# Where one transfer stands in a convolution kernel: the kept rows of VectorE's layout, written behind the next shifts of the 3x3 part

## The chip, the cores and the metric

The kernel runs on one core of a Trainium2 chip. The time is device microseconds of one execution of the whole program; the time of a kernel is the median of its runs. The core has TensorE (PE, matrix products), VectorE (DVE), ScalarE (ACT), GpSimd (POOL) and SyncE (SP). They run at the same time, each through its own list of instructions in order, and wait for each other by semaphores. SP and POOL issue the transfers (DMAs); SP does nothing else here.

## What is computed

`x` holds 8 images of 32 channels and 128 x 128 pixels, in float32. Layer 0 normalises them by groups, finds for every pixel the 8 most similar of 25 shifted copies, gathers those into 256 channels, and runs them through three pairs of a 1x1 and a 3x3 depthwise convolution. Layer 1 is a 5x5 convolution.

```
xb = _patch_match_stack(x)                      # [8, 256, 128, 128]
dct = _conv(xb, dct_w, groups=C)
h = relu(_conv(_conv(xb, w1), w2, groups=CK, pad=1))
h = relu(_conv(_conv(h, w3), w4, groups=CK, pad=1))
wiener = sigmoid(_conv(_conv(h, w5), w6, groups=CK, pad=1))
filt = _conv(wiener * dct, inv_dct_w, groups=C)
...
x = x + _L0_conv_ref(_gn(x), ...)
x = x + _L1_conv_ref(_gn(x), L1_conv_kernel, 1, 2)
```

The change concerns the 3x3 depthwise convolutions (`w2`, `w4`, `w6`).

## The kernel before

**Steps and phases.** An image is cut into strips of 8 rows; a step handles one strip, and each image has 16 strips and a last short one (`n == NS`), so 17 steps, 136 in all. In every step the main loop passes through four phases, `i` = 3, 2, 1, 0. Phases 3, 2 and 1 run a stage, that is one pair of 1x1 and 3x3 convolutions, each on a strip that entered a step later than the one before; phase 0 multiplies by the `dct` part and closes a strip. The gathering of pixels, the block matching for the next image (task queues drained by `run` and `tick`) and layer 1 are spread between.

**Two layouts for a 3x3 part.** A stage has 256 channels. The first 128 go through PE: `pointwise_t` makes the 1x1 part into the tile `t` (one for each stage), ACT copies it from PSUM (L668), and two transfers on SP's queue, L671 and L673, shift rows between partitions so that PE finds the three neighbouring rows side by side. `depthwise_t` then does the nine taps as 48 small matmuls (L709). The second 128 go through DVE: `pointwise_v` makes the 1x1 part, ACT copies it into `tv` (L646), `depthwise_v` does the centre tap on ACT (L686) and the eight others on DVE (L689), then the activation function on ACT (L693).

**Rows kept from strip to strip.** A 3x3 part needs two rows of the strip above. `rows_before_t` (L617) and `rows_before_v` (L624) transfer them inside `t` and `tv`: for `tv`, rows 8 and 9 go to rows 0 and 1. Both are on SP's queue. At the end of an image they write zeros on POOL instead (L619, L626). The taps of a strip must have read rows 0 and 1 before they are overwritten, and L646 of the next strip must not write rows 2 to 9 before rows 8 and 9 are read.

**How the pieces of a phase are written.** `depthwise_v` and `depthwise_t` are generators; the main loop takes a piece of each at a time. In phase `i`, in this order: `pointwise_v` of the stage and the centre tap; the eight taps on DVE (`next(new_v, None)`); `pointwise_t` with its shifts; the matmuls L709 of the stage of the phase before (`next(dt, None)`), after the gathering matmuls or, in phase 0, ahead of them; then the end of the stage of the phase before: `next(dv, None)` gives L693 and the kept rows of `tv`, `next(dt, None)` gives ACT's L721 and the kept rows of `t`.

**What sets the order.** The loop stands under a manual schedule for PE, DVE and ACT: these three run in the written order. SP and POOL are not in that set:

```
ORDERED = {mybir.EngineType.PE, mybir.EngineType.DVE, mybir.EngineType.Activation}
...
    with tc.manual_schedule(engines=ORDERED):
```

Their order is made by the framework's planner, which knows what each instruction reads and writes and in which order all were written, and which also sets the semaphores.

Of the kernel before, what the change touches and what calls it, by code (L numbers as in the profile page):

```python
# [43 lines left out]
def bm3d_conv_preact(  # L44
# [171 lines left out]
    def push(task):  # L216
        want = next(task, None)
        if want:
            which, cost, *wait = want
            queues[which].append((cost, task, now[0] + (wait[0] if wait else 0)))  # L220
# [400 lines left out]
    def rows_before_v(i, b, n):  # L621
        v = tv[i - 1]
        if n < NS:
            nc.sync.dma_start(v[:, 0:2], v[:, R : R + 2])  # L624
        else:
            nc.gpsimd.memset(v[:, 0 : i + 1], 0.0)  # L626
# [21 lines left out]
    def pointwise_t(i, b, n, lhsT, src):  # L648
        t = tb[i - 1]
        nb = 2 if n < NS else 1  # L650
        if n == NS and i == 1:
            nc.gpsimd.memset(t[:, :, 2], 0.0)
        else:
            for q in range(2):
                ps = ps_x.tile([P, 2, 2, W], F32, name=f"p{i}_{b}_{n}_{q}", tag="x")
                for e in range(2):
                    s = slice(C * (2 * q + e), C * (2 * q + e + 1))
                    for g in range(2):
                        rows = src(g)
                        for r in range(4):  # L660
                            nc.tensor.matmul(  # L661
                                ps[C * r : C * (r + 1), e, :nb],
                                lhsT[:, g, s],
                                rows[:, r : r + 4 * nb - 3 : 4],
                                start=g == 0,
                                stop=g == 1,
                            )
                nc.scalar.copy(t[:, 2 * q : 2 * q + 2, 2 : 2 + nb], ps[:, :, :nb])  # L668
            for r in range(i - 1) if n == 0 else range(i - 1, 4) if n == NS else ():
                nc.gpsimd.memset(t[C * r : C * (r + 1), :, 2], 0.0)  # L670
        nc.sync.dma_start(t[64:P, :, 0:nb], t[0:64, :, 2 : 2 + nb])  # L671
        if nb == 2:
            nc.sync.dma_start(t[0:64, :, 1], t[64:P, :, 2])  # L673

    def depthwise_v(i, b, n):
        v = tv[i - 1]
        nr = R if n < NS else 4
        out_ = accp.tile([P, R, W], F32, name=f"acc{i}_{b}_{n}_1", tag=f"acc{i}1")
        acc = out_[:, :nr]
        for k, (dy, dx) in enumerate(  # L680
            ((1, 1), (0, 0), (0, 1), (0, 2), (1, 0), (1, 2), (2, 0), (2, 1), (2, 2))
        ):
            tap = dwv[:, i - 1, 3 * dy + dx : 3 * dy + dx + 1]
            rows = v[:, dy : dy + nr, dx : dx + W]
            if k == 0:
                nc.scalar.activation(acc, rows, AF.Copy, scale=tap)  # L686
                yield out_
            else:
                nc.vector.scalar_tensor_tensor(  # L689
                    acc, rows, tap, acc, op0=ALU.mult, op1=ALU.add  # L690
                )
        yield
        nc.scalar.activation(acc, acc, funcs[i - 1])  # L693
        rows_before_v(i, b, n)

    def depthwise_t(i, b, n):
# [28 lines left out]
    def final_load(b, n):  # L725
        j0, j1 = (3, R) if n == 0 else (0, R if n < NS else 3)
        ya, yz = R * n - 3 + j0, R * n - 3 + j1

        whole = j1 - j0 == R
        nr, nw = (2, W) if whole else (j1 - j0, C)  # L730
        xr = work.tile([P, 2 * W], F32, name=f"xr_{b}_{n}", tag="xr")
        xr = xr[:, : nr * nw].rearrange("p (r w) -> p r w", w=nw)
        for j in range(4):
            ra = ya + 2 * j if whole else ya
            xa = 0 if whole else C * j
            nc.gpsimd.dma_start(
                xr[C * j : C * (j + 1)], x[b, :, ra : ra + nr, xa : xa + nw]
            )

        xf = xbp.tile([P, 2, R, W], F32, name=f"xf_{b}_{n}", tag="xf", bufs=1)  # L740
        src = xbd[b].rearrange("(j m c) g y x -> g m j c y x", j=4, m=2)
        for g in range(2):
            for m in range(2):
                nc.gpsimd.dma_start(
                    xf[64 * g : 64 * (g + 1), m, j0:j1], src[g, m, :, :, ya:yz]
                )
        return xr, xf, j0, j1
# [119 lines left out]
    def unit(stage, u):  # L867
        if 0 <= u < len(units) and units[u]:
            stage(*units[u])

    def source(i, b, n):
        src = xbs.pop((b, n), None) if i == 1 else accs.pop((i - 1, b, n))
        return (lambda g: src[:, g]) if i == 1 else (lambda g: src[g])
# [9 lines left out]
    def tick(i):  # L883

        now[0] += 1
        owed[0] += total / (NS - 2) * (0.4 if i == 0 else 0.2)
        owed[0] -= run("D", owed[0]) if owed[0] > 0 else 0
        owed[0] = min(owed[0], 6.0)

    def until(cond, credit):  # L890
        while not cond():
            now[0] += 1
            run("D", credit)
            run("A")
            run("P")
            run("Q")

    with tc.manual_schedule(engines=ORDERED):
        push(prep(0))
        push(mixes())  # L900
        until(lambda: 0 in ready, 4.0)
        xbd[0] = dram.tile([P, 2, H, W], F32, name="xbd_0", tag="xbd")
        for i in range(3):
            nc.gpsimd.memset(tb[i][0:64, :, 0], 0.0)
        for u in range(7):
            unit(gather_load, u)
            unit(gather_select, u - 2)
            unit(gather_pixels, u - 3)
        u = 4

        dt = dv = iter(())

        later = lambda: None

        for s in range(len(steps) + 2):
            if s < len(steps):
                b, n = steps[s]
                if s == 2:
                    push(bands())
                if n == 0 and b + 1 < NB:  # L920
                    push(prep(b + 1))
                if n == NS - 1 and b + 1 < NB:
                    until(lambda: b + 1 in ready, 4.0)
                    xbd[b + 1] = dram.tile([P, 2, H, W], F32, name=f"xbd_{b+1}", tag="xbd")
            for i in (3, 2, 1, 0):
                si = s - (i - 1 if i else 2)
                live = 0 <= si < len(steps)
                new_v = new_t = iter(())
                if live:
                    bi, ni = steps[si]  # L930

                if live and i:
                    src = source(i, bi, ni)
                    pointwise_v(i, bi, ni, lws[i - 1], src)
                    new_v, new_t = depthwise_v(i, bi, ni), depthwise_t(i, bi, ni)
                    accs[i, bi, ni] = [None, next(new_v)]
                later()
                later = lambda: None
                if live and not i:
                    if ni == 0:  # L940
                        x1d[bi] = dram.tile([C, H, W], F32, name=f"x1d_{bi}", tag="x1d")
                        stats[bi] = work.tile([P, NS + 1, 6], F32, name=f"stat_{bi}", tag="stat")
                    xr, xf, j0, j1 = fins.pop(si)
                run("P")
                if live and not i:
                    final_dct(bi, ni, accs[3, bi, ni], xf, j0, j1)

                run("Q")
                if s < len(steps):
                    unit(gather_select, u + 1)  # L950
                    unit(gather_load, u + 3)
                    tick(i)
                next(new_v, None)
                if live and i:
                    pointwise_t(i, bi, ni, lws[i - 1], src)
                if not i:
                    next(dt, None)
                if s < len(steps):
                    unit(gather_pixels, u)
                    u += 1  # L960
                if i:
                    next(dt, None)
                run("A")
                next(dv, None)
                next(dt, None)
                dv, dt = new_v, new_t
                if live and not i:
                    later = partial(end, bi, ni, xr, j0, j1)
                if not i and 0 <= s - 1 < len(steps):
                    fins[s - 1] = final_load(*steps[s - 1])  # L970
        later()
        until(lambda: NB - 1 in done, 4.0)

# [61 lines left out]
```

## Time and profile before

| | us |
|---|---|
| median of 3 runs | 7167.68 (7158.68 to 7188.37) |
| profiled execution | 7169.27 |
| its span, first to last instruction | 7167.5 |
| DVE taps, L689, 3264 of them | 4083.7 busy, 1.252 each |
| PE 3x3 matmuls, L709, 19584 of them | 2174.5 busy |
| shifts L671 and L673 with kept rows L617, issue to landing | 4.9 median |
| kept rows L624, issue to landing | 4.0 median, 2.0 to 12.4 |

A line of the waits view tells who waited and in which line, after the arrow what ended the wait, then microseconds in total, how many times, and the longest. "SPq" is the queue of SP: its instructions wait in order, so one that waits holds all that stand behind it. A line of the timeline gives start, duration, engine, line, operation and tiles; "x8" means eight instructions merged. The groups' busiest lines read thus:

```profile
L689 DVE SCALAR_TENSOR_TENSOR acc<-tv,dwv,acc 128x1024 f32<-128x1024 f32 (+1 forms) x3264 | 4083.7, 1252 | 214.6 <-ACT acc L686 103.2
L709 PE MATMUL pw<-t,dwd 128*32 128x508 f32 (+6 forms) x19584 | 2174.5, 591 | 151.3 <-DMA t<-t 116.0
```

That is busy time and mean duration in ns, then the idle time ahead of the group and what ended most of it.

### The profile page before, as it was taken

How to read it: one execution, taken by the hardware profiler on the slowest of the kernel's cores; microseconds unless marked ns; L12 is line 12 of the kernel's file. 1: busy time of each engine (PE TensorE's matmuls, PEld its weight loads, DVE VectorE, ACT ScalarE, POOL GpSimd, SP SyncE). 2: the span in 40 equal slices, each digit the busy share in tenths (PEclk: the TensorE clock that was granted, in tenths of full speed). 3: DMA queues.
4: the chain of work that ended last, by engine and by line, in shares of the span. 5: the costliest groups of instructions: out<-in, count | busy, mean ns of one | idle time of the engine just before them, and what ended most of it. 6: DMA issues, size and time to landing. Idle time of an engine off the chain costs nothing. (4 is left out here: it accounts for less than half of the span.)

```text
span 7167.5 us, 229467 instructions
## 1 busy us (share of the span) xinstructions
PE 6709.5 (94%) x100226; PEld 3178.5 (44%) x100226; DVE 5835.6 (81%) x8606; ACT 5061.9 (71%) x6704; POOL 2716.4 (38%) x4599
## 2 busy tenths in 40 slices
PE   4699999999999999999999999999999999999997
PEld 1344444444444444444444444444444444444443
DVE  7689878788788888888888888888888889767675
ACT  4777668677686777767677776877668677676662
POOL 6343335333353333533344333543335333232222
PEclk7799999999999999999999999999999999999999
DMA  3476656667566665756656565666656655556652
GB/s 82 120 163 146 149 136 152 139 148 152 131 157 143 141 152 125 165 147 138 151 125 160 141 149 134 144 156 147 148 134 143 161 137 148 129 148 140 143 136 63
DMA packets 762413, 1007.47 MB, mean 141 GB/s; under 512 B 211425, under 2 KB 575009, under 8 KB 761409
## 3 DMA queue, kind: packets, MB, share of 16 engines
q0 software_dynamic: 375328, 733.44, 42.2%
q1 hardware_dynamic: 381056, 256.86, 17.1%
q8 instruction: 788, 12.91, 0.8%
q10 hardware_dynamic: 5024, 2.49, 0.2%
q14 instruction: 217, 1.77, 0.1%
HBM read 542.24 MB, written 217.01 MB: 106 GB/s over the span
## 5 line engine op out<-in xcount | busy, mean ns | idle before, releaser
L689 DVE SCALAR_TENSOR_TENSOR acc<-tv,dwv,acc 128x1024 f32<-128x1024 f32 (+1 forms) x3264 | 4083.7, 1252 | 214.6 <-ACT acc L686 103.2
L709 PE MATMUL pw<-t,dwd 128*32 128x508 f32 (+6 forms) x19584 | 2174.5, 591 | 151.3 <-DMA t<-t 116.0
L709 PEld LDWEIGHTS pw<-t,dwd 128*32 128x32 f32 (+1 forms) x19584 | 702.9, 111 | 1384.1 <-issue 1182.2
L571 POOL DMA_DIRECT2D ib<-idxd x1024 | 570.9, 558 | 1803.4 <-ACT sel L586 1611.8
L585 ACT ACTIVATE ib<-ib,nplace 128x1024 bf16<-128x1024 bf16 x1024 | 1165.5, 1138 | 16.6 <-DMA ib<-idxd 16.6
L586 ACT ACTIVATE sel<-ib 128x1024 f32<-128x1024 bf16 x1024 | 1084.4, 1059 | 32.6
L661 PE MATMUL p<-acc,lw 128*32 128x256 f32 x17408 | 994.6, 375 | 20.2 <-issue 20.2
L638 PE MATMUL pv<-acc,lw 128*128 128x512 f32 (+1 forms) x2112 | 979.8, 607 | 8.0 <-DVE acc L760 3.9
L607 ACT COPY xb<-pg 128x512 f32<-128x512 f32 x512 | 303.9, 594 | 732.8 <-PE pg L600 732.6
L646 ACT COPY tv<-pv 128x512 f32<-128x512 f32 (+2 forms) x784 | 445.6, 584 | 493.6 <-PE pv L638 483.1
L661 PEld LDWEIGHTS p<-acc,lw 128*32 128x32 f32 x17408 | 565.2, 110 | 441.2 <-issue 99.6
L600 PEld LDWEIGHTS pg<-sel,xt 128*32 128x32 f32 x45056 | 594.8, 111 | 226.2 <-issue 142.7
L721 ACT ACTIVATE acc<-pw 128x512 f32<-128x512 f32 (+1 forms) x816 | 453.3, 585 | 341.1 <-PE pw L709 340.6
L780 DVE TENSOR_TENSOR xr<-xr,pa 128x256 f32<-128x256 f32 (+2 forms) x136 | 55.0, 405 | 765.2 <-PE pa L773 757.3
L600 PE MATMUL pg<-sel,xt 128*32 128x48 f32 x45056 | 598.0, 206 | 84.8 <-issue 69.3
L638 PEld LDWEIGHTS pv<-acc,lw 128*128 128x128 f32 x2112 | 383.9, 193 | 409.8 <-issue 379.2
L411 DVE TENSOR_TENSOR df<-xn 128x786 f32<-128x786 f32 (+2 forms) x576 | 528.7, 967 | 22.1 <-PE pd L426 20.6
L668 ACT COPY t<-p 128x512 f32<-128x512 f32 x800 | 423.8, 571 | 113.3 <-PE p L661 110.1
L686 ACT ACTIVATE acc<-tv,dwv 128x1024 f32<-128x1024 f32 (+1 forms) x408 | 459.8, 1127 | 49.5 <-PE pa L773 32.3
L419 ACT ACTIVATE df<-df 128x786 f32<-128x786 f32 (+2 forms) x576 | 459.6, 862 | 24.5 <-DVE df L411 23.9
L638 PE MATMUL pv<-xb,lw 128*128 128x512 f32 x1024 | 474.8, 606 | 0.0
L757 PE MATMUL pc<-xf,ldct 128*128 128x512 f32 (+2 forms) x1056 | 472.0, 589 | 0.0
(128 smaller groups left out, 6366.3 us busy)
## 6 DMA issues: line engine op xcount, KB each, us to landing
ib<-idxd POOLq DMA_DIRECT2D x1024, 256.0 KB, 4.4
xbd<-xb POOLq DMA_DIRECT2D x128, 1024.0 KB, 8.6
xf<-xbd POOLq DMA_DIRECT2D x480, 256.0 KB, 10.1
t<-t SPq DMA_DIRECT2D x792, 128.0 KB, 4.9
t<-t SPq DMA_DIRECT2D x384, 256.0 KB, 4.9
tv<-tv SPq DMA_DIRECT2D x384, 130.0 KB, 4.0
xt<-xtd POOLq DMA_DIRECT2D x240, 176.0 KB, 5.2
xl<-xs POOLq DMA_DIRECT2D x256, 64.0 KB, 2.5
```

The source lines that it names most:

```text
L411: nc.vector.tensor_sub(df[:, :, ca:cz], xn[:, r0 : r0 + SR, ca:cz], xn[:, r0 + dy : r0 + dy + SR, ca + dx : cz + dx],)
L419: nc.scalar.activation(df[:, :, ca:cz], df[:, :, ca:cz], AF.Square)
L571: nc.gpsimd.dma_start(ib.rearrange("p k y x -> p (k y x)"), idxd[b][s4, 4 * k0 : 4 * k0 + 8] .rearrange("k x -> (k x)") .partition_broadca ...
L585: nc.scalar.activation(ib, ib, AF.Square, bias=nplace)
L586: nc.scalar.activation(sel, ib, AF.Relu, scale=-1.0, bias=1.0)
L600: nc.tensor.matmul(pg[C * j : C * (j + 1), :, xa:xz], xt[:, t], sels[j // 2][:, j % 2, :, xa:xz], start=True, stop=True,)
L638: nc.tensor.matmul(ps[:, :hr], lhsT[:, g, P:CK], src(g)[:, h : h + hr], start=g == 0, stop=g == 1,)
L661: nc.tensor.matmul(ps[C * r : C * (r + 1), e, :nb], lhsT[:, g, s], rows[:, r : r + 4 * nb - 3 : 4], start=g == 0, stop=g == 1,)
L686: nc.scalar.activation(acc, rows, AF.Copy, scale=tap)
L689: nc.vector.scalar_tensor_tensor(acc, rows, tap, acc, op0=ALU.mult, op1=ALU.add)
L709: nc.tensor.matmul(pt[u][C * j : C * (j + 1), :, :nb, xa:xz], dwd[0:hi, i - 1, u, j, dx + 1], t[0:hi, j, :, :nb, xa + dx : xz + dx], start ...
L757: nc.tensor.matmul(ps[:, : z - a], ldct[:, m], xf[:, m, a:z], start=True, stop=True)
```

## The change

`depthwise_v` stops once more between its activation and the transfer of the kept rows. The main loop keeps the generator for one more phase, in `kept`, and takes its last piece there behind `pointwise_t`. The zeros of `tv` at the end of an image move in the same way. Nothing is computed differently.

```
@@ -691,6 +691,7 @@
         yield
         nc.scalar.activation(acc, acc, funcs[i - 1])
+        yield
         rows_before_v(i, b, n)
@@ -908,7 +909,7 @@
-        dt = dv = iter(())
+        dt = dv = kept = iter(())
@@ -953,6 +954,7 @@
                 next(new_v, None)
                 if live and i:
                     pointwise_t(i, bi, ni, lws[i - 1], src)
+                next(kept, None)
                 if not i:
                     next(dt, None)
@@ -963,11 +965,12 @@
                 next(dv, None)
                 next(dt, None)
-                dv, dt = new_v, new_t
+                kept, dv, dt = dv, new_v, new_t
                 if live and not i:
                     later = partial(end, bi, ni, xr, j0, j1)
...
+        next(kept, None)
         later()
         until(lambda: NB - 1 in done, 4.0)
```

In written order, the SP queue of a step was, phase by phase (the number is the stage):

| phase | before | after |
|---|---|---|
| 3 | L671, L673 (3) | L671, L673 (3), L624 (1, of the step before) |
| 2 | L671, L673 (2), L624 (3), L617 (3) | L671, L673 (2), L617 (3) |
| 1 | L671, L673 (1), L624 (2), L617 (2) | L671, L673 (1), L624 (3), L617 (2) |
| 0 | L624 (1), L617 (1) | L624 (2), L617 (1) |

More of the change, by code (lines that the diff above doesn't have):

```diff
@@ L693, in depthwise_v @@
         nc.scalar.activation(acc, acc, funcs[i - 1])
+        yield
         rows_before_v(i, b, n)
@@ L909, in bm3d_conv_preact @@
         u = 4
-        dt = dv = iter(())
+        dt = dv = kept = iter(())
         later = lambda: None
@@ L955, in bm3d_conv_preact @@
                     pointwise_t(i, bi, ni, lws[i - 1], src)
+                next(kept, None)
                 if not i:
@@ L965, in bm3d_conv_preact @@
                 next(dt, None)
-                dv, dt = new_v, new_t
+                kept, dv, dt = dv, new_v, new_t
                 if live and not i:
@@ L970, in bm3d_conv_preact @@
                     fins[s - 1] = final_load(*steps[s - 1])
+        next(kept, None)
         later()
```

## The prediction

> **What bounds the kernel now.** I read the head of the page first, for the busiest engine.
>
> ```profile
> span 7167.5 us, 229467 instructions
> PE 6709.5 (94%) x100226; PEld 3178.5 (44%) x100226; DVE 5835.6 (81%) x8606; ACT 5061.9 (71%) x6704; POOL 2716.4 (38%) x4599
> ```
>
> TensorE (PE) is busy for 6709.5 of 7167.5 us. So a change can gain at most the 458.0 us in which PE idles, and it can gain only where it ends such an idle time. The view of waits, kept to PE, tells what ends them: microseconds in total, times, longest.
>
> ```profile
> PE pw L709 <- DMA t<-t: 116.0, 63, 8.0
> ...
> PE pw L709 <- DMA tv<-tv: 8.9, 5, 2.7
> ```
>
> The largest is the 3x3 part on PE (L709) waiting for a transfer within `t`, the layout that PE reads. The transfer that is moved here, within `tv`, ends only 8.9 us. In ScalarE's (ACT's) L646, which overwrites the rows that it reads, it ends 4.5 us more (the waits listed for the tile `tv`).
>
> Next came the same view for SP, whose queue issues all of these transfers.
>
> ```profile
> SPq L617 <- PE pw L709: 1292.0, 261, 18.0
> SPq L624 <- DVE acc L689: 1093.5, 290, 14.1
> ```
>
> The reader is to see that L624 stands at the head of SP for 1093.5 us, waiting for taps (L689) of VectorE (DVE). That is odd. As written, L624 follows L693, a whole phase after its taps, and should find them done. The timeline of a piece of one step explains it.
>
> ```profile
> 4036.05 10.51 DVE L689 SCALAR_TENSOR_TENSOR acc<-tv,dwv,acc 128x1024 f32<-128x1024 f32 x8
> ...
> 4042.30 0.59 ACT L668 COPY t<-p 128x512 f32<-128x512 f32 x1 [1.14 <-PE p L661]
> 4042.67 0.50 SPq L624 DMA_DIRECT2D tv<-tv  x1
> ...
> 4043.26 0.59 SPq L671 DMA_DIRECT2D t<-t  x1
> 4043.91 0.62 SPq L673 DMA_DIRECT2D t<-t  x1
> ...
> 4053.84 0.59 SPq L671 DMA_DIRECT2D t<-t  x1
> ...
> 4054.48 0.61 SPq L673 DMA_DIRECT2D t<-t  x1
> 4055.68 1.06 ACT L693 ACTIVATE acc<-acc 128x1024 f32<-128x1024 f32 x1
> 4056.51 0.50 SPq L624 DMA_DIRECT2D tv<-tv  x1
> ```
>
> The eight taps are those of stage 3. Five of them (dy 0 and dy 1) read rows 0 to 8; the transfer overwrites rows 0 and 1, so it must wait for the fifth. That ends at 4036.05 + 5/8 x 10.51 = 4042.62, and L624 goes at 4042.67. It goes even before the shifts of the same stage (4043.26), 11 us before those of stage 2 (4053.84) and 13 us before its own L693 (4055.68), all of which are written ahead of it. **So SP does not keep the written order.** The code holds only PE, ACT and DVE to theirs (`ORDERED`, L898); the framework's planner puts SP's instructions where their data come free. I matched all 384 transfers to their taps, by stage and step: the time from the end of the fifth tap to the issue has a median of 0.0 us, is under 1 us in 95 of 100, and 4.1 us at most.
>
> **The change, part by part.** It removes and adds no instruction. *The yield after L693:* ACT keeps its order, since nothing of ACT's stands in what is moved; 0 us. *The 384 transfers:* each takes SP 0.502 us as before (384 x 0.502 = 193 us, on a queue that is mostly waiting). In the text each moves behind the same stage's L617 and behind L671 and L673 of the stage two phases on, where there are such. What it needs is the same, since nothing between the two places touches its `tv`, so its data come free at the same tap. If the planner goes on issuing what is ready, SP's order changes only where two issues become ready together and the written rank decides. Of 384 transfers, 9 are followed at once on SP by an L617 of their own stage. Even there a swap costs one 0.59 us issue on either side, at most 9 x 0.59 = 5 us of SP's time, and the L617 rows are needed a step later. *The 24 zeroings (L626, on POOL, at the ends of images):* 0.43 us each, needed by the next image's L686, which comes 32 us or more after them in the 21 cases that have one. POOL's other work stands behind them; they now rank behind it. I take 0. *The last call, after the loop,* finds nothing left: the last strip of stage 3 hands over its zeroing one phase after its L693, still inside the loop; 0. No wait is added. Sum: 0.
>
> Should the transfers truly move to their written places, the trace shows no such run, so I bound the effect from both sides. *Gain at the head of SP:* in 195 places an L671 follows an L624. Its lag after the ACT copy that it needs adds up to 31.7 us, counting lags above 0.2 us (32 of them). Set beside the idle time of the L709 that reads the rows, only 0.6 us of it reaches PE: a shift goes 6 to 12 us ahead of that matmul in the median of each stage, and this covers a lag of a few. *Gain on the DMA engines:* of 338 second shifts (L673) whose landing is known, 253 have a row transfer issued between 3 us before them and 0.5 us before their landing; PE idles 108.9 us ahead of their matmuls, 0.43 each. The other 85 have 11.8 us, 0.14 each. If all became like the others: 108.9 - 253 x 0.14 = 74 us. *Loss:* the rows would come later for the next L646 and L686. At the written place with the median landing of 4.0 us, the smallest slack left is 8.3 us for stage 3, 9.9 for stage 2, 6.9 for stage 1, so nothing waits. With the longest landing of all, 12.4 us, every time, 35 of them would be late, by 21.7 us together. This cover gone, ACT, then the taps, then PE wait. So the unknown lies between -74 and +22 us; I take 0, because the row nearest to it, the transfer that goes 0.0 us after its tap wherever it is written, says that it stays.
>
> A page and this row: SP's 1093.5 us of waiting sits in the queue itself, ahead of the issue. The Trainium skill (DMA: Bandwidth & Descriptors, section on the anatomy of one DMA) says the same in general: a semaphore wait happens on the issuing sequencer, and the DMA engines only consume their queues. By that rule alone, all that is queued behind L624 is held for up to 1093.5 us, and moving it away would be worth that much; by the lags it is worth 31.7 us at SP and 0.6 at PE.
>
> **Sum.** The profiled execution took 7169.27 us, 1.8 more than its span, and is 1.6 above the median of the runs shown, 7167.68. With a sum of 0, I forecast the median: **7168 us**.
>
> **Rivals.** *Unlocked shifts (faster).* The transfers do move, off the DMA engines while shifts are under way. At most 7168 - 74 = 7094 us; with half of it, 7131. For it: 116.0 us of PE waits for `t`. Against: in the written order a row transfer still follows right behind a shift (stage 3's behind those of stage 1), so they overlap again; and the trace has the planner reaching ahead.
>
> *POOL takes the zeroings badly (slower).* Place: the ends of images, where the L626 would sit in POOL's in-order queue ahead of gather loads, blocked on taps not yet due. Their sister L632 does so now:
>
> ```profile
> POOL tv L632 <- DVE acc L689: 264.9, 16, 25.8
> POOL tv L626 <- DVE acc L689: 40.3, 11, 6.1
> ```
>
> Around one such block of 25.5 us (981 to 1007) PE stays fully busy, 26.00 of 26.00 us, and idles 0.50 + 1.97 = 2.5 us in the 52 us after it. 24 x 2.5 = 59 us gives 7227 us. It decides once a zeroing blocks POOL for some 25 us instead of the 3.7 (40.3/11) of now. Against: a later rank lets other work pass rather than block.
>
> *Late rows (slower, slightly).* The loss above: 7168 + 22 = 7190. It decides once a landing takes 4.0 + 6.9 = 10.9 us; 99 of 100 now take less.
>
> *The change does nothing to SP* is my forecast itself.
>
> **How the numbers follow.** About 0.5% (36 us) is what a measurement of this kernel can tell from no change; the three runs shown spread over 30 us. Order unchanged: 0.74, of which 0.70 within that bound and 0.02 beyond it on either side. Unlocked shifts: 0.12, of which 0.08 beyond it. POOL: 0.10, all slower. Late rows: 0.04, of which 0.01 beyond. Faster 0.02 + 0.08 = 0.10; same 0.70 + 0.04 + 0.03 = 0.77; slower 0.02 + 0.10 + 0.01 = 0.13. The forecast's own range is that of the runs, 7155 to 7190. I reach from 7125, just past half of the unlocked gain, to 7215, most of the way to POOL's 7227; that leaves out some 0.07 below and 0.08 above.
>
> **What would show it.** Right: SP's waits at L624 for L689 stay near 1093 us over some 290 times; L624 still goes at the fifth tap, ahead of later shifts; PE's wait for `t` stays near 116 us; PE busy stays near 6710. Wrong towards faster: L624 stands behind L671 and L673 with no DVE wait, and PE's 116.0 shrinks. Wrong towards slower: POOL's wait at L626 grows from 40.3 to hundreds, or ACT's L646 waits for `tv` far above 4.5 us. If the planner reaches only so far ahead of the written order, or if a few swapped issues shift its whole plan for POOL, the prediction is wrong.

## The result and the profile after

Before: 7166.15 us median of 14 runs (7147.25 to 7200.13). After: 7168.12 us median of 14 runs (7147.54 to 7191.91). The ratio is 1.0002, with a 95% interval of 0.9987 to 1.0018: no difference that can be measured. Ratios here and below count fast executions alone; one of the twelve with SP held and the new place (below), 11884.64 us at a granted clock of 0.654, is left out.

The profiled execution after has a span of 7175.7 us. The lines that answer to those shown of before, first from its page (busy time, share, instructions):

```profile
span 7175.7 us, 229467 instructions
PE 6719.3 (94%) x100226; PEld 3184.0 (44%) x100226; DVE 5837.8 (81%) x8606; ACT 5061.0 (71%) x6704; POOL 2716.5 (38%) x4599
```

From its view of waits, for SP (who waited for whom, us in total, times, longest):

```profile
SPq L617 <- PE pw L710: 1287.6, 255, 17.4
SPq L624 <- DVE acc L689: 1097.4, 293, 14.1
```

and for PE:

```profile
PE pw L710 <- DMA t<-t: 109.7, 53, 7.9
...
PE pw L710 <- DMA tv<-tv: 5.0, 5, 2.4
```

and for POOL:

```profile
POOL tv L632 <- DVE acc L689: 264.6, 16, 25.8
...
POOL tv L626 <- DVE acc L689: 39.3, 11, 6.1
```

The large ones of these waits are those of before, within 6% (the 3x3 matmuls are L710 now, being one line lower). SP still waits some 1100 us at L624, in 293 places instead of 290, for taps that would be long done at the written place. ACT's wait for `tv` at L646 is 10.2 us instead of 4.5. The timeline of the step that was shown of before, in the changed kernel:

```profile
4040.82 10.52 DVE L689 SCALAR_TENSOR_TENSOR acc<-tv,dwv,acc 128x1024 f32<-128x1024 f32 x8
...
4047.43 0.50 SPq L624 DMA_DIRECT2D tv<-tv  x1
...
4048.03 0.59 SPq L671 DMA_DIRECT2D t<-t  x1
4048.67 0.61 SPq L673 DMA_DIRECT2D t<-t  x1
...
4058.59 0.59 SPq L671 DMA_DIRECT2D t<-t  x1
```

The fifth tap ends at 4040.82 + 5/8 x 10.52 = 4047.40, and the transfer goes at 4047.43, again ahead of the shifts of its own stage (4048.03) and 11 us ahead of those of the next (4058.59). In the text it now stands behind both, and behind those of stage 1 as well. Matched over all 384 transfers as before, the time from the fifth tap to the issue is 0.03 us in the median of each stage, in both kernels.

The programs themselves go further than the trace: the instructions of the two, laid side by side, are the same on all five engines, in the same order and with the same semaphores to wait for; only line numbers and the numbers in names differ. The change is one of the text alone. What was measured is one program against itself. So the interval of 0.9987 to 1.0018 shows how finely 14 runs can tell, and the differences between the two profiles are scatter: 116.0 and 109.7 us for PE's wait for `t`, 4.5 and 10.2 for ACT's wait for `tv`.

### The profile page after: what moved, and what is told of

Same layout as the page of the kernel before. It is cut to its first block, busy times and chain, and to the rows that moved or that the text cites. A ratio compares the mean times of both kernels' runs of the same rounds, so it can differ in the third digit from the quotient of the medians.

```text
span 7175.7 us, 229467 instructions
## 1 busy us (share of the span) xinstructions
PE 6719.3 (94%) x100226; PEld 3184.0 (44%) x100226; DVE 5837.8 (81%) x8606; ACT 5061.0 (71%) x6704; POOL 2716.5 (38%) x4599
## 5 line engine op out<-in xcount | busy, mean ns | idle before, releaser
L710 PE MATMUL pw<-t,dwd 128*32 128x508 f32 (+6 forms) x19584 | 2182.3, 593 | 144.9 <-DMA t<-t 109.7
L710 PEld LDWEIGHTS pw<-t,dwd 128*32 128x32 f32 (+1 forms) x19584 | 703.4, 111 | 1384.0 <-issue 1200.9
L585 ACT ACTIVATE ib<-ib,nplace 128x1024 bf16<-128x1024 bf16 x1024 | 1165.5, 1138 | 20.6 <-DMA ib<-idxd 20.6
L586 ACT ACTIVATE sel<-ib 128x1024 f32<-128x1024 bf16 x1024 | 1084.6, 1059 | 32.6
L638 PE MATMUL pv<-acc,lw 128*128 128x512 f32 (+1 forms) x2112 | 978.0, 606 | 11.9 <-DVE acc L761 7.6
L646 ACT COPY tv<-pv 128x512 f32<-128x512 f32 (+2 forms) x784 | 444.9, 584 | 496.4 <-PE pv L638 474.7
L638 PEld LDWEIGHTS pv<-acc,lw 128*128 128x128 f32 x2112 | 383.5, 192 | 412.2 <-issue 377.0
L668 ACT COPY t<-p 128x512 f32<-128x512 f32 x800 | 423.5, 570 | 117.9 <-PE p L661 114.6
L638 PE MATMUL pv<-xb,lw 128*128 128x512 f32 x1024 | 475.1, 607 | 0.0
## 6 DMA issues: line engine op xcount, KB each, us to landing
xf<-xbd POOLq DMA_DIRECT2D x480, 256.0 KB, 10.1
```

Of the source, the lines that this page charges most:

```text
L585: nc.scalar.activation(ib, ib, AF.Square, bias=nplace)
L586: nc.scalar.activation(sel, ib, AF.Relu, scale=-1.0, bias=1.0)
L638: nc.tensor.matmul(ps[:, :hr], lhsT[:, g, P:CK], src(g)[:, h : h + hr], start=g == 0, stop=g == 1,)
L710: nc.tensor.matmul(pt[u][C * j : C * (j + 1), :, :nb, xa:xz], dwd[0:hi, i - 1, u, j, dx + 1], t[0:hi, j, :, :nb, xa + dx : xz + dx], start ...
```

## Experiments

Two questions are left. Does the planner ignore the written place elsewhere too, and what would the place be worth if it were kept? Ratios below are to the kernel before, timed on the same chip, with 95% intervals.

### Written still later, left to the planner

```
-        rows_before_v(i, b, n)
+        owing[i] = partial(rows_before_v, i, b, n)
...
+                    owing.pop(i, lambda: None)()
                     src = source(i, bi, ni)
                     pointwise_v(i, bi, ni, lws[i - 1], src)
```

> The kernel before with L624 written as late as it may stand, directly ahead of the next pointwise_v of its stage, four phases after its taps, and SP left to the planner (the zeroings at the very last image end, which nobody reads, are left out). Theory (SP goes by data, not by the text): L624 still goes at its fifth tap, SP waits there for L689 about 1093 us over some 290 times, ratio 0.998 to 1.002. Rival (the planner reaches only so far ahead, and the change lay within its reach): L624 goes later, its wait for L689 falls under 500 us, and L646 begins to wait for tv.

Measured: ratio 1.0013 (0.9999 to 1.0028). Its waits on SP:

```profile
SPq L617 <- PE pw L709: 1318.1, 259, 18.1
SPq L624 <- DVE acc L689: 1086.9, 288, 14.1
```

The transfer goes 0.03 us after its fifth tap in the median, though its text stands four phases after it. SP's order is the same again, transfer by transfer, and so is that of PE, ACT and DVE. PE's wait for `t` is 121.5 us here: three profiles with one order on SP span 109.7 to 121.5. So the rival, that the change only happened to lie within the planner's reach, falls: even the last place allowed does not move the transfer.

### SP held to the written order: the old place

```
-ORDERED = {mybir.EngineType.PE, mybir.EngineType.DVE, mybir.EngineType.Activation}
+ORDERED = {
+    mybir.EngineType.PE,
+    mybir.EngineType.DVE,
+    mybir.EngineType.Activation,
+    mybir.EngineType.SP,
+}
```

> The kernel before, with SP added to the engines that must keep the written order, so each L624 stands behind L671 and L673 of the next phase. Theory (the planner had put L624 at its fifth tap, and place is worth little): SP's wait at L624 for L689 falls from 1093 us to under 100; the time stays within the bounds of the prediction, 7168 - 74 to 7168 + 22 us, likeliest a ratio of 0.997 to 1.003. Rival 'unlocked shifts': PE's 116 us of waits for t falls by half or more, ratio near 0.990. Rival 'late rows': L646 waits for tv far above 4.5 us, ratio above 1.003.

Measured: ratio 0.9986 (0.9974 to 0.9999). Two waits of SP, at the first shift (L676 here, five lines lower than L671) and at the transfer (L629, for the taps L694), and PE's wait for the shifts:

```profile
SPq L676 <- ACT t L673: 1142.7, 103, 17.7
...
SPq L629 <- DVE acc L694: 185.4, 208, 6.2
```

```profile
PE pw L714 <- DMA t<-t: 112.5, 54, 8.3
```

The transfer now stands at its written place. It goes 9.0 us (stage 3), 11.6 us (stage 2) and 0.8 us (stage 1) after the fifth tap in the median. SP's wait fell from 1093.5 to 185.4 us, where under 100 was expected. PE's wait for `t` stays, 112.5 against 116.0. Some 908 us less of waiting at this transfer go with at most 0.26% of the time. SP's queue as a whole does not wait less: the shift's wait for ACT's copy of `t` grew from 543.0 to 1142.7 us, and all lines of the view add up to 6259 us against 6233. The waiting only moved from one instruction of an in-order queue to others. As the edit orders all of SP's instructions, the 0.9986 is not the price of this transfer's place alone.

### SP held to the written order: the new place

The changed kernel with the same edit.

> The changed kernel with SP held to the written order in the same way: this is the change as its text says it, L624 one phase later again. Theory: against the run with SP held and the old place, within 0.3%; the rows still come 7 us or more before they are overwritten, so L646 waits for tv under 20 us in all. Rival 'unlocked shifts': 0.5 to 1% faster than that run, with PE's wait for t lower by 35 us or more. Rival 'late rows': up to 22 us slower, seen as L646 or L686 waiting for tv.

Measured: ratio 1.0010 (0.9993 to 1.0026). Against the run with SP held and the old place that is 1.0010 / 0.9986 = 1.0024, and the two intervals overlap, so a small loss is likely and not settled. It lies within the 0.3% that was expected. The transfer goes 23.5, 14.0 and 23.8 us after the fifth tap in the median of stages 3, 2 and 1. SP and PE there:

```profile
SPq L629 <- DVE acc L694: 93.4, 161, 1.8
```

```profile
PE pw L715 <- DMA t<-t: 107.6, 61, 7.8
...
PE pw L715 <- DMA tv<-tv: 17.1, 6, 3.3
```

PE's wait for the shifts did not fall by 35 us, so the rival "unlocked shifts" fails where it should have shown. From landing to the next L646 of the stage, the slack in the median is 10.1, 19.4 and 9.3 us, and 4.2 us at the least; L646 does not wait for `tv` in this trace at all. So the rival "late rows", by its sign at L646, has not set in either. PE's waits put down to the row transfer itself are 17.1 us in 6 places, against 2.6 with SP held and the old place and 8.9 before. Together with those for `t` that is 124.7 against 115.1 us, 9.6 us more; but it is 114.7 to 128.6 in the three profiles with one order on SP, so this does not settle the small loss.

### SP held, the latest place: the cover taken away

The two edits, the latest place and SP held, together.

> The same latest place, with SP held to the written order: the cover of 7 us and more is gone, since the issue comes about when pv starts and the first L646 follows 1.9 us after that, while the rows land 4.0 us after their issue. Theory: L646 waits for tv some 2 to 3 us in most of 384 strips, 700 to 1000 us of waits on ACT, of which ACT's idle share (29%) hides a part: ratio 1.01 to 1.08. Rival (place is worth nothing at all, wherever it is): ratio within 0.3% of 1.

Measured: 7888.89 us, ratio 1.0994 (1.0967 to 1.1021). The waits of ACT and PE:

```profile
ACT tv L651 <- DMA tv<-tv: 1404.7, 298, 10.7
...
ACT acc L691 <- DMA tv<-tv: 92.4, 17, 8.2
```

```profile
PE pw L714 <- DMA t<-t: 395.0, 152, 11.2
PE pg L605 <- issue: 64.2, 39, 6.1
PE pg L605 <- ACT tv L651: 59.8, 29, 4.9
```

Here the mechanism of "late rows" shows itself: L651 (L646 of before) waits for the rows in 298 places, 4.7 us each instead of the 2 to 3 that I expected, and the time grows by more than my 1 to 8%. The waits on ACT add up to 1404.7 + 92.4 = 1497.1 us, and the time grew by 719 us, about half of that (7888.89 against 7170.13). Each wait is longer than I estimated for two reasons that the trace shows. The landing got slower (5.1 us in the median instead of 4.0). And the transfer goes later than "about when pv starts": in the median 4.5 us behind the first matmul of `pv` in stage 2 and 2.9 in stage 1 (0.1 us ahead of it in stage 3). A part of the way to PE is visible: ACT is in order, so the copies of `t` that stand behind L651 on ACT go late too, and PE's wait for `t` grows from 116.0 to 395.0 us. SP is not what holds these shifts: they go 0.03 us after ACT's copy in the median, and in none of the places where PE waits for them more than 0.2 us after it. Of the 727 us by which the span grew, PE idles in 488 (458.0 to 945.6) and is busy for 239 more (6709.5 to 6948.5) with the same instructions. The granted clock is lower as well in these executions, 0.95 against 0.976; what lowers it is open.

### No transfer, and two of them

The first leaves the transfer of the rows out, so that rows 0 and 1 of `tv` are stale; the second writes it twice in a row.

```
-            nc.sync.dma_start(v[:, 0:2], v[:, R : R + 2])
+            pass
```

```
             nc.sync.dma_start(v[:, 0:2], v[:, R : R + 2])
+            nc.sync.dma_start(v[:, 0:2], v[:, R : R + 2])
```

> The kernel before without the transfer L624 (384 transfers of 130 KB left out, so the first two rows of each strip in tv are stale; zeroing stays). It bounds what any place of it can gain. Theory: it costs PE next to nothing, ratio 0.997 to 1.001. Rival 'unlocked shifts': the idle time of PE ahead of L709 falls by up to 74 us, ratio near 0.990.

> The kernel before with L624 issued twice in a row (384 more transfers of 130 KB at the same place). Theory: SP has room, ratio 0.999 to 1.004. Rival 'unlocked shifts', by which a row transfer near a shift costs PE 0.29 us: 253 x 0.29 = 74 us more, ratio 1.010, with PE's wait for t near 190 us.

Measured: without it 0.9976 (0.9964 to 0.9989); twice 1.0000 (0.9984 to 1.0016). PE's wait for the shifts without it:

```profile
PE pw L709 <- DMA t<-t: 100.1, 50, 8.4
```

and with two, where SP also waits for the first before it issues the second:

```profile
SPq L625 <- DMA tv<-tv: 1163.2, 376, 12.0
SPq L624 <- DVE acc L690: 999.1, 296, 14.1
```

```profile
PE pw L710 <- DMA t<-t: 113.6, 60, 9.0
```

Leaving out all 384 transfers is worth 0.24%, 17 us (8 to 26 by the interval), inside what was expected and far from the 74 us of the rival. PE's wait falls by 15.9 us, to 9.6 us below the least of the three profiles with one order on SP. Twice as many cost nothing that can be measured, though the second always goes after the first has landed. With no transfer at all worth 17 us, no place of it is likely to gain more.

### What does bound this stretch: the shifts behind ACT's selection

PE's wait for `t` stays between 100 and 122 us in all of the runs above, but for the one that made ACT late. In the timeline of before, ACT copies `t` (L668) right after four selection instructions (L585, L586):

```profile
4048.50 1.13 ACT L585 ACTIVATE ib<-ib,nplace 128x1024 bf16<-128x1024 bf16 x1
4049.66 1.06 ACT L586 ACTIVATE sel<-ib 128x1024 f32<-128x1024 bf16 x1
4050.63 1.13 ACT L585 ACTIVATE ib<-ib,nplace 128x1024 bf16<-128x1024 bf16 x1
4051.79 1.06 ACT L586 ACTIVATE sel<-ib 128x1024 f32<-128x1024 bf16 x1
4052.76 1.05 ACT L668 COPY t<-p 128x512 f32<-128x512 f32 x2
```

So I moved `pointwise_t` ahead of the selection in the text of ACT and PE, whose order is kept. The edit for stage 1 is this; that for all three stages has `if live and i` at the new place and nothing at the old one.

```
                 later()
                 later = lambda: None
+                if live and i == 1:
+                    pointwise_t(i, bi, ni, lws[i - 1], src)
...
                 next(new_v, None)
-                if live and i:
+                if live and i > 1:
                     pointwise_t(i, bi, ni, lws[i - 1], src)
```

> An attempt on the wait that does cost PE, 116 us for t: the kernel before with pointwise_t of stage 1 written ahead of the selection work of its phase, so that ACT copies t (L668) before L585 and L586 and the shifts go some 4 us earlier. Theory (stage 1's shifts are late behind ACT's selection): PE's wait for t falls from 116 to about 40 us, ratio 0.988 to 0.996. Rival (the gain is given back: taps or selection come later and PE waits for ACT): ratio 0.998 or more, with waits for L586 grown.

> The same for all three stages. Theory: PE's wait for t falls below 40 us, ratio 0.986 to 0.996. Rival: stages 3 and 2 have slack already (their L709 idle only 38 and 19 us), so nothing more comes than with stage 1 alone, and the copies ahead of the selection delay it: ratio within 0.3% of that with stage 1 alone, or above.

Measured: stage 1 alone 7130.80 us, ratio 0.9941 (0.9922 to 0.9960); all three stages 7089.74 us, ratio 0.9888 (0.9870 to 0.9907). PE's waits with stage 1 alone:

```profile
PE pg L600 <- issue: 70.7, 35, 4.9
PE pw L709 <- DMA t<-t: 48.7, 27, 4.8
```

and with all three:

```profile
PE pg L600 <- issue: 75.5, 37, 5.2
PE pw L709 <- DMA t<-t: 34.5, 16, 6.3
```

The copy now goes ahead of the selection, here with all three stages:

```profile
4054.13 0.57 ACT L668 COPY t<-p 128x512 f32<-128x512 f32 x1
4055.55 0.59 ACT L668 COPY t<-p 128x512 f32<-128x512 f32 x1 [0.85 <-PE p L661]
4056.04 1.15 ACT L585 ACTIVATE ib<-ib,nplace 128x1024 bf16<-128x1024 bf16 x1
```

With stage 1 alone, the time from the end of ACT's copy to the first L709 grows from 6.9 to 9.8 us in the median of that stage, and PE's idle time ahead of these matmuls falls from 83.2 to 9.8 us; the medians of stages 3 and 2 stay at 8.2 and 11.5. With all three they are 10.3 and 14.4 as well.

With all three stages the wait fell by 116.0 - 34.5 = 81.5 us, and 1.12% of 7170 is 80 us. PE's whole idle time, span less busy time, fell from 458.0 to 7095.6 - 6716.7 = 378.9 us, so nearly all of it came out of the time. What was given back is small: PE's wait for the selection, L586, is 16.9 us against 15.5, and its wait at L638 for the products of DVE's L760 is 25.0 against 3.9. The rival for all three, that stages 3 and 2 have nothing more to give, falls: they gave another 0.5%, 41 us. Of these, 14 us show in the wait for `t` (48.7 to 34.5); where the rest comes from is open. With SP's text untouched and the same transfers, an earlier producer did what moving a neighbour of the shifts in the text could not. Both kernels of this case are slower than this one.

## Why the prediction was right

*SP does not keep the written order, and data say when the transfer goes.* Right, and shown twice: the program of the changed kernel is that of before, and even the latest place gives the same list on SP. That the forecast of 7168 met 7168.12 so closely is luck: the same program gave medians of 7166.15 and 7168.12, and its executions span 53 us.

*Up to nine issues might swap by rank.* None did. There the bound was safe and not needed, and the 24 zeroings kept their places on POOL as well; POOL's wait at L626, the mark of the slower rival, could not grow.

*The gain at the head of SP, 31.7 us of lags and 0.6 us at PE.* Right in kind: the waiting at L624 costs next to nothing. With SP held at the old place, 908 us of it left L624, other instructions of SP waited as much longer, and at most 0.26% came of it (0.14%, 10 us, in the middle of the interval; the 0.6 us themselves are too small to be tested). Here the waits of the queue are no measure of what is lost by them; the lag of what stands behind them, against its slack, came closer.

*The gain on the DMA engines, up to 74 us.* This term was mis-sized. Taking the transfer out is worth 17 us, and doubling it nothing. The difference of 0.43 and 0.14 us was put down to the neighbour without a run that showed it. Of the 108.9 us, 65.7 stand ahead of the matmuls of stage 1, and all of that stage's idle time there, 83.2 us, falls only to 74.4 with no row transfer at all, but to 9.8 with ACT's copy ahead of the selection. So what decides there is how long before the matmul ACT copies `t`. Where the row transfer did move (SP held, new place), PE's wait for `t` was 107.6, and the kernel was no faster.

*Late rows: 22 us at most, since 6.9 us or more of slack remain.* Right for the place that was proposed, in that nothing waits at L646. The smallest slack came out at 4.2, 14.5 and 4.4 us for stages 3, 2 and 1, where 8.3, 9.9 and 6.9 had been worked out with one landing time for all: for stages 3 and 1 about half and two thirds of it. With the cover gone the price is 9.9%, not tens of microseconds, where the rows are issued only as the next strip begins.

*The chances.* The 0.26 that I left to a moved order was caution: all 384 transfers of the trace before already went by their taps.

## What to carry to other kernels

Before costing a move in the text, see in the trace whether that engine keeps the text's order: find the instruction, find the last event that it needs, and measure the time between them. If it is zero everywhere, and the instruction goes ahead of others that are written before it, the text's place is not what sets it, and the wait shown ahead of it is only the queue waiting for data. Then look for what PE waits for, and move its producer on an engine whose order is kept.

## What the runs showed beyond that

A planner's order by readiness and the written order are worth the same here for SP's 1598 transfers: 0.9986 (0.9974 to 0.9999) with the queue held to the text. What looked like a blocked queue of 1093.5 us hid a cost of 0.26% at most, and with the queue held SP waited as long in all, 6259 us against 6233, at other instructions.

A late transfer made others late through an in-order engine. With 1497.1 us of waits for `tv` on ACT the time grew by 719 us, and PE's wait for the transfers of the other layout more than tripled (116.0 to 395.0 us), though these went 0.03 us after ACT's copy as before.
